# A graph-attention layer on one core: 29 pairs of raw rows instead of 24, with twelve row buffers and reordered group steps

## The chip, the cores and the metric

The kernel runs on one core of a Trainium2 chip. The metric is the time on the device in microseconds (us), from start to end of one execution; lower is better. The engines are called by the names of the profile: PE (TensorE, matrix products), DVE (VectorE), ACT (ScalarE), POOL (GpSimd) and SP (SyncE, which here only issues DMAs). Each engine works through its own queue of instructions in order, and waits on semaphores for others. "L897" is line 897 of the kernel before.

## The reference

`x` has 12500 nodes of 128 features, and there are 400000 edges, sorted by destination, with 32 attributes each. One layer of GATv2 attention with 8 heads and a feed-forward block is computed:

```python
h = relu(layernorm(x))
n1 = ln1(h)
x_l, x_r = n1 @ W_l, n1 @ W_r                    # 8 heads of 16
m = leaky_relu(x_l[src] + x_r[dst] + edge_attr @ W_e, 0.2)   # also one loop per node, with the mean attribute
alpha = einsum('ehc,hc->eh', m, att)
a = softmax of alpha over the edges of each dst
g = h + segment_sum(x_l[src] * a, dst) + bias
out = x + g + gelu(ln2(g) @ W1 + b1) @ W2 + b2
```

## The kernel before, in words

Nodes lie in 98 tiles of 128. Edges are cut into 782 pairs; a pair is two units of 256 edges, so four blocks of 128 edges. The program has a front, a main loop over pairs, and an end. Every order is written out by hand: functions are called round by round under a manual schedule, and each engine's queue has that order.

**The front** (from `make_identity` to `clear(0)`, rounds `r` at L720) loads `x`, normalizes it in groups of four tiles, and writes the rows `x_l` to DRAM (`x_l`, L526 and L534). One group enters per round, and `x_l` of a group comes 8 rounds after it entered. Beside this, three more things are done in the front:

- *Raw rows.* For 24 pairs, one in every 32, `raw_gather` (L268) gathers the rows of `x` by source with four indirect DMAs, issued by POOL, into a tile `raw` with five buffers; three rounds later `raw_store` (L279) stores them through SP to `raw_dram`. Their indices come with one load, `load_raw`.
- *Differences.* `from_first` (L387) turns the destinations into float (`df`), subtracts the first destination of each unit and of each pair on POOL (`dlb`, L392), and stores both tables to DRAM for the main loop. `fits` (L400) computes a flag that the edges have the expected shape; `edge_constants` (L346) builds constants on DVE out of loaded weights, in round 7.
- The row of `x_r` for the first group (`first_xr`).

**The main loop** (`window_edges`, round loop at L1321) handles a pair `c` in stages, one round apart: `gather` (L889) four rounds ahead, `combine` (PE sums z, L939 to L943), `slope` and `bend`, `score`, `lowest`, `weigh` (ACT exponentials), `turn` (PE), `keep_turned` (ACT), `collect` (PE, L1001), `own_heads` (DVE, L1010 and L1016, seven rounds after `combine`), and `put` (L1023), which stores the two units' sums through SP to `state`. `gather` normally issues four indirect DMAs on POOL (L897), each fetching 128 rows of `x_l`. The tile `xs` has 12 buffers, and a buffer becomes free when `collect` has read it. For one of the 24 raw pairs, `gather` is a plain load from `late_dram` through SP instead, and the twelve `raw_steps`, one per round, have computed the pair's `x_l` rows from the raw rows before (on DVE, ACT and PE). `xr_steps` compute `x_r` for a group of four tiles, eight rounds long, once in about 32 rounds. In the first 196 rounds the mean edge attribute is also summed up (`sum_load`, `sum_up`), and the state is cleared in parts.

When all edges of a group of four node tiles are done, the group's steps run, one or more per round, from round `d["round"]` on: `f_load` (0) loads state, `x_l` and `x_r`; then `f_order`, `f_z`, `f_bend`, `f_score`, `f_low` (5), which needs the state, and so on to `f_up`, `f_gelu`, `f_down` (18) and `f_store` (19), which computes the output and issues its store. Groups are at least 23 rounds apart. The last one but one begins in round 764, the last one in round 790, when all 782 pairs have been put.

In each round the calls stand in this order: `f_gelu(1)`, the pair's stages, the sums, the clearing, the steps of groups, `xr_steps`, `raw_steps`, then

```python
        late_stages = (
            (-WAHEAD, windows),
            (LATE + 2, put),
        )
```

so SP finds `put` last, after the loads for the pair three rounds ahead (`windows`, L905 to L918).

Of the kernel before, what the change touches and what calls it, by code (L numbers as in the profile page):

```python
# [13 lines left out]
F32 = mybir.dt.float32  # L14
BF16 = mybir.dt.bfloat16
I32 = mybir.dt.int32
AF = mybir.ActivationFunctionType
OP = mybir.AluOpType
# [3 lines left out]
P = 128  # L22
# [3 lines left out]
K = 4  # L26
# [7 lines left out]
KU = 2  # L34
U = KU * P
UP = 2
# [12 lines left out]
AHEAD = 4  # L49
WAHEAD = 3  # L50
XR_STEPS = 8
RAW_STEPS = 12
BIG = 2.0**126
CAP = 2.0**120
# [50 lines left out]
def edges_per_node(nt, n_edges):  # L105
    return -(-n_edges // (nt * P))
# [7 lines left out]
def xr_round(t0, nt, n_edges):  # L114

    first = (t0 * P - CW) * edges_per_node(nt, n_edges) // U - SPARE
    return first // UP - WAHEAD - XR_STEPS - 1


def raw_pairs(nt, n_edges):  # L120

    n_pr = -(-n_edges // (UP * U))
    at = [xr_round(t, nt, n_edges) + XR_STEPS + 1 for t in range(GN, nt, GN)]
    return [(r + RAW_STEPS + AHEAD + 1, r) for r in at if r + RAW_STEPS + AHEAD + 2 < n_pr]


# [9 lines left out]
def tile_gnn(  # L136
# [118 lines left out]
    src_raw = build.tile([P, len(raw), UP * KU], I32, name="src_raw")  # L255

    def load_raw():
        step = raw[1]["c"] - raw[0]["c"]
        assert all(d["c"] == raw[0]["c"] + i * step for i, d in enumerate(raw))
        nc.sync.dma_start(  # L260
            src_raw,
            bass.AP(
                tensor=src.tensor, offset=src.offset + raw[0]["c"] * UP * KU,
                ap=[[NCH * K, P], [step * UP * KU, len(raw)], [1, UP * KU]],
            ),
        )

    def raw_gather(d):  # L268
        d["x"] = node.tile([P, UP * KU, P], F32, name="raw", bufs=5)
        for j in range(d["n"]):  # L270
            nc.gpsimd.indirect_dma_start(  # L271
                out=d["x"][:, j, :],
                out_offset=None,
                in_=x,
                in_offset=bass.IndirectOffsetOnAxis(ap=src_raw[:, d["i"], j : j + 1], axis=0),
            )
# [97 lines left out]

    df = rng.tile([RP, EP + U + 1], F32, name="df")
    bad = rng.tile([RP, 2], F32, name="bad")

    def last_of_units():
        nc.vector.tensor_copy(lu, dc[:, U - 1 : EP : U])

        u = NUE - 1
        nc.sync.dma_start(
            lu[u // RU : u // RU + 1, u % RU : u % RU + 1],
            bass.AP(tensor=dst.tensor, offset=dst.offset + n_edges - 1, ap=[[0, 1], [1, 1]]),
        )

    def from_first():  # L387
        nc.vector.tensor_copy(df, dc)
        for step, to in ((U, du_dram), (UP * U, dc_dram)):
            de = df[:, 0:EP].rearrange("p (u e) -> p u e", e=step)  # L390
            dlb = rng.tile([RP, EP], BF16, name="dlb", bufs=2)
            nc.gpsimd.tensor_tensor(  # L392
                dlb.rearrange("p (u e) -> p u e", e=step),
                de,
                de[:, :, 0:1].to_broadcast([RP, EP // step, step]),
                op=OP.subtract,
            )
            nc.sync.dma_start(to.rearrange("(p e) -> p e", e=EP), dlb)

    def fits():  # L400
# [303 lines left out]
    with tc.manual_schedule():  # L704
        make_identity(nc, ident)
        count_up()
        for t in xls:
            nc.gpsimd.memset(t[:, :, P:], 1.0)
        load_weights()
        load_x(0, min(GN, NT))  # L710
        load_raw()
        load_x(GN, min(3 * GN, NT - GN))
        for t in range(4 * GN, NT, 14):
            load_x(t, min(14, NT - t))
        load_dst()
        load_consts()
        nc.gpsimd.memset(empty, 0.0)
        nc.gpsimd.memset(empty[:, :, C + 1 : SH], CAP)
        rows_at = [i * 5 // 4 + (3 if i >= 10 else 0) for i in range(len(raw))]
        for r in range(max(max(len(qs), 9) + LAST + 1, rows_at[-1] + 4)):  # L720
            for d, at in zip(raw, rows_at):
                if r == at:
                    raw_gather(d)
                if r == at + 3:
                    raw_store(d)
            if r == 3:
                weights()
            if r == 7:
                edge_constants()
            if r == 8:  # L730
                last_of_units()
            if r == 12:
                from_first()
            if r == 14:
                fits()
            for t in slots(r - 2):
                nc.vector.reciprocal(t, t)
            for t in slots(r - 1):
                nc.scalar.activation(t, t, AF.Sqrt)
            for late, f in node_stages:  # L740
                if 0 <= r - late < len(qs):
                    f(qs[r - late], r)
            if 0 <= r - LAST < len(first_xr):
                first_xr[r - LAST](qs[0])
        clear(0)
# [82 lines left out]
def window_edges(  # L828
# [30 lines left out]
    with ExitStack() as es:  # L859
# [192 lines left out]
        def tiles(name, d, tag=None, bufs=1):  # L1052
            d[name] = fin.tile([P, GN, P], F32, name=f"f_{name}", tag=tag or f"f_{name}", bufs=bufs)
            return d[name][:, 0 : d["n"]]
# [2 lines left out]
            d[name] = ps2.tile([P, EPR], F32, name=ring)  # L1057
            return d[name]

        def f_load(d):  # L1060
            n, ts = d["n"], d["ts"]
            d["st"] = fin.tile([P, 2, GN, SW], F32, name="st", tag="big", bufs=3)
            for i in range(2):
                nc.sync.dma_start(d["st"][:, i, 0:n], state[i].rearrange("(t p h) f -> p t (h f)", p=P, h=H)[:, ts, :])
            d["xl"] = fin.tile([P, GN, XW], F32, name="f_xl")
            nc.sync.dma_start(d["xl"][:, 0:n], xl_t[:, ts, :])
            d["xr"] = fin.tile([P, GN, NS, P], BF16, name="f_xr")
            nc.sync.dma_start(d["xr"][:, 0:n], xs_t[:, ts, :, :])
# [150 lines left out]
        def f_gelu(k):  # L1219
            def gelu(d):  # L1220
                n = d["n"]
                if k == 0:
                    d["gel"] = fin.tile([P, 2, GN * P], F32, name="gel", tag="big", bufs=3)
                nc.scalar.activation(
                    d["gel"][:, k, 0 : n * P], d[f"u{k}"][:, 0 : n * P], AF.Gelu, bias=cols[:, 5 + k : 6 + k]
                )

            return gelu
# [12 lines left out]

        def f_store(d):
            n = d["n"]
            y = tiles("yo", d, "f_b")
            up = d["y"][:, 0 : n * P].rearrange("p (t f) -> p t f", f=P)
            nc.vector.tensor_add(up, up, d["x"][:, 0:n])
            nc.vector.tensor_add(up, up, h_sb[:, d["ts"], :])
            nc.vector.tensor_add(y, up, b2_r[:, None, :].to_broadcast([P, n, P]))  # L1248
            nc.sync.dma_start(out_t[:, d["ts"], :], y)

        stages = (
            (-AHEAD, gather),
# [11 lines left out]
        )  # L1264
        late_stages = (
            (-WAHEAD, windows),
            (LATE + 2, put),
        )
        sum_stages = (
            (0, sum_load),  # L1270
# [1 line left out]
            (3, mean),  # L1272
        )
        SUM_STEP = 2
        early = ((17, f_gelu(1)),)
        steps = (
            (0, f_load),
            (1, f_order),
            (2, f_z),
            (3, f_bend),  # L1280
            (4, f_score),
            (5, f_low),
            (6, f_exp),
            (7, f_den),
            (8, f_out),
            (9, f_h),
            (10, f_stats),
            (11, f_root),
            (12, f_scale),
            (13, f_turn),  # L1290
            (14, f_turned),
            (15, f_up(0)),
            (16, f_up(1)),
            (16, f_gelu(0)),
            (18, f_down),
            (19, f_store),
        )
        GAP = 23
        last_round = n_pr + LATE + 2
        free = SUM_STEP * (NL - 1) + 5  # L1300
        for d, u in zip(groups, done_after(NT, n_edges)):
            d["round"] = max(free, (u // UP if u < NUE else n_pr) + LATE + 2)
            free = d["round"] + GAP
# [14 lines left out]

        CLEAR = 8
        with tc.manual_schedule():  # L1320
            for r in range(-AHEAD, max(last_round, groups[-1]["round"] + 20)):  # L1321
                in_round(r, early)
                for late, f in stages:
                    c = r - late
                    if 0 <= c < n_pr:
                        f(c)
                for late, f in sum_stages:
                    i, off = divmod(r - late, SUM_STEP)
                    if off == 0 and 0 <= i < NL:
                        f(i)  # L1330
                if r > 0 and r % CLEAR == 0 and r // CLEAR < NT // GT:
                    clear(r // CLEAR)
                in_round(r, steps)
                in_round(r, enumerate(xr_steps), qs[1:])
                in_round(r, enumerate(raw_steps), raw)
                for late, f in late_stages:
                    c = r - late
                    if 0 <= c < n_pr:
                        f(c)
# [358 lines left out]
```

## Time and profile before

| what | value |
|---|---|
| median of 3 runs | 4033.95 us (4027.9 to 4034.51) |
| the profiled execution: time, span | 4031.16 us, 4029.0 us |
| busy in the span: PE, DVE, ACT, POOL | 3542.0, 2539.1, 2131.2, 2980.9 us |
| mean granted clock of PE | 0.954 |
| front: start of the first raw gather, start of the last | 6.33, 164.08 us |
| main loop: start of the first gather, of the last | 168.53, 3959.64 us |
| last sum of the last pair begins | 3982.61 us |
| output store of the last group issued | 4023.75 us |

The profile is one execution recorded by the hardware. Its span runs from the first to the last instruction; the time of the execution is some 2 us longer. Busy time of an engine says what it executed, and not what it waited for. For a gather on POOL the record covers the work of issuing, not the landing of the data.

### The profile page before, as it was taken

Reading aid. Unit: us, or ns where it says so; the run is one execution under the profiler, and the core shown is the slowest. Engines: PE = TensorE matmul, PEld = TensorE weight load, DVE = VectorE, ACT = ScalarE, POOL = GpSimd, SP = SyncE. Lnnn points to the kernel's source line nnn. Section 1 sums busy time; section 2 is a strip of 40 time slices with the busy share of each in tenths; the row PEclk is TensorE's granted clock in tenths of the full one; section 3 lists DMA queues with packets and bytes.
Section 4 is the critical chain, followed back from the end, with each engine's and each line's share of the span. In section 5 each row is a group of like instructions: output and inputs, shape, how many; then the busy total and the mean of one; then the engine's idle time right before and its main releaser. Section 6 shows DMA issues by size and latency. Waiting matters only on the chain.

```text
span 4029.0 us, 65580 instructions
## 1 busy us (share of the span) xinstructions
PE 3542.0 (88%) x19059; PEld 2507.7 (62%) x19255; DVE 2539.1 (63%) x5835; ACT 2131.2 (53%) x4638; POOL 2980.9 (74%) x3155
## 2 busy tenths in 40 slices
PE   3488888888899999999999999989999999989986
PEld 2356666666666666666666666666666666666664
DVE  6556666666666666666666666666666665656654
ACT  5544544544455555555465456555555555545553
POOL 6777777777777777777777777777777777777772
PEclk7799999999999999999999999999999999999998
DMA  6778878767666666656666666656666666566562
GB/s 185 207 175 192 193 184 190 174 160 168 164 120 137 124 124 132 125 112 131 131 126 131 126 132 124 128 127 115 124 136 126 125 131 130 111 131 112 120 133 56
DMA packets 646655, 560.85 MB, mean 139 GB/s; under 512 B 384830, under 2 KB 523949, under 8 KB 646045
## 3 DMA queue, kind: packets, MB, share of 16 engines
q1 hardware_dynamic: 545709, 339.00, 33.7%
q0 software_dynamic: 100000, 217.41, 30.4%
q8 instruction: 156, 2.56, 0.3%
q14 instruction: 214, 1.75, 0.2%
q10 hardware_dynamic: 576, 0.13, 0.0%
HBM read 489.80 MB, written 66.32 MB: 138 GB/s over the span
## 4 chain that ended last, share of the span: by engine, by line
PE 38%; POOL 25%; DMA 22%; issue 13%; SPq 1%; DVE 1%; ACT 0%; POOLq 0%; DVEq 0%; ACTq 0%
POOL xs L897 23%; DMA xs<-xl_dram,src_sb 21%; PE z L943 8%; PE acc L1001 8%; PE ab L961 7%; PE pt_ps L987 4%; PE z L939 4%; PE z L942 2%; POOL raw L271 2%; PE ab L960 1%; PE acc L1234 1%; PE acc L1209 1%; SPq L283 0%; DMA state<-rec 0%; DMA dc<-in_dst 0%
## 5 line engine op out<-in xcount | busy, mean ns | idle before, releaser
L897 POOL DMA_INDIRECT xs<-xl_dram,src_sb x3029 | 2868.9, 947 | 923.3 <-issue 792.7
L979 ACT ACTIVATE p<-ab,rec 128x256 f32<-128x256 f32 x1563 | 655.5, 471 | 1055.2 <-DVE rec L968 1039.1
L1010 DVE TENSOR_TENSOR own<-acc,diag 128x272 f32<-128x272 f32 x782 | 343.6, 439 | 1049.5 <-PE acc L1001 1034.9
L1001 PE MATMUL acc<-xs,pt 128*128 128x136 f32 x6250 | 879.8, 285 | 0.2 <-DVE f_yo L1248 0.2
L939 PE MATMUL z<-ident,xs 128*128 128x128 f32 x3125 | 562.6, 283 | 349.9 <-DMA xs<-xl_dram,src_sb 319.2
L939 PEld LDWEIGHTS z<-ident,xs 128*128 128x128 f32 x3125 | 398.7, 142 | 756.6 <-DMA xs<-xl_dram,src_sb 419.8
L943 PE MATMUL z<-ea,we_z 128*128 128x512 f32 x1564 | 839.4, 619 | 0.1
L961 PE MATMUL ab<-m,negrep 128*128 128x512 f32 x1564 | 799.5, 593 | 11.0 <-issue 1.1
L1001 PEld LDWEIGHTS acc<-xs,pt 128*128 128x128 f32 x6250 | 807.1, 196 | 0.4 <-PE pt_ps L987 0.4
L992 ACT COPY pt<-pt_ps 128x512 f32<-128x512 f32 x782 | 455.1, 582 | 619.5 <-PE pt_ps L987 613.8
L987 PEld LDWEIGHTS pt_ps<-ident,p 128*128 128x128 f32 x3125 | 408.6, 146 | 440.8 <-issue 391.2
L968 DVE TENSOR_REDUCE rec<-ab 128x2 f32<-128x512 f32 x781 | 539.7, 691 | 121.8 <-PE ab L961 113.3
L954 DVE TENSOR_TENSOR m<-z,zs 128x512 f32<-128x512 f32 x782 | 532.6, 681 | 127.4 <-ACT zs L949 127.0
L949 ACT ACTIVATE zs<-z 128x512 f32<-128x512 f32 x782 | 472.6, 604 | 41.1 <-DMA ea<-in_ea_t 32.2
L987 PE MATMUL pt_ps<-ident,p 128*128 128x128 f32 x3125 | 490.2, 281 | 1.9 <-ACT p L979 0.9
L1016 DVE TENSOR_REDUCE rec<-own 128x34 f32<-128x272 f32 x782 | 340.9, 436 | 26.7
L943 PEld LDWEIGHTS z<-ea,we_z 128*128 128x128 f32 x1564 | 308.0, 197 | 33.1
L961 PEld LDWEIGHTS ab<-m,negrep 128*128 128x128 f32 x1564 | 300.8, 192 | 37.4 <-issue 1.1
L942 PE MATMUL z<-ne,xrw 128*128 128x512 bf16 (+1 forms) x781 | 305.0, 391 | 0.2 <-issue 0.2
L925 DVE TENSOR_SCALAR ne<-dlw,nid 112x512 bf16<-112x512 bf16 x782 | 290.7, 372 | 14.0 <-DMA dlw<-du_dram 13.9
L960 PE MATMUL ab<-ne,farw 128*128 128x512 bf16 x588 | 225.4, 383 | 0.0
L271 POOL DMA_INDIRECT raw<-in_x,src_raw x96 | 95.6, 996 | 53.3 <-issue 28.5
(198 smaller groups left out, 2232.9 us busy)
## 6 DMA issues: line engine op xcount, KB each, us to landing
dlw<-dc_dram SPq DMA_DIRECT2D x196, 384.0 KB
ea<-in_ea_t SPq DMA_DIRECT2D x196, 256.0 KB
ea_s<-in_ea_t SPq DMA_DIRECT2D x98, 512.0 KB
xs<-xl_dram,src_sb POOLq DMA_INDIRECT x3029
state<-rec SPq DMA_DIRECT2D x1563, 9.0 KB
xrw<-xs_dram SPq DMA_DIRECT2D x782, 24.0 KB
state<-empty SPq DMA_DIRECT2D x28, 504.0 KB
st<-state SPq DMA_DIRECT2D x48, 288.0 KB
```

The source lines that it names most:

```text
L897: nc.gpsimd.indirect_dma_start(out=xs[:, j, :], out_offset=None, in_=xl_dram, in_offset=bass.IndirectOffsetOnAxis(ap=src_sb[:, c * KP + j ...
L939: nc.tensor.matmul(z[:, j * P : (j + 1) * P], d["xs"][:, j, 0:P], ident, start=(j == 0), stop=False, is_transpose=True)
L942: nc.tensor.matmul(z[:, :e], xrw[c % NV], d["ne"][:, :e], start=False, stop=False)
L943: nc.tensor.matmul(z[:, :e], we_z[:, c % QP, :], d["ea"][:, :e], start=False, stop=True)
L949: nc.scalar.activation(d["zs"][:, :e], d["z"][:, :e], AF.Copy, scale=SLOPE)
L954: nc.vector.tensor_tensor(d["m"][:, :e], d["z"][:, :e], d["zs"][:, :e], op=OP.max)
L961: nc.tensor.matmul(ab[:, :e], negrep.rearrange("p n h -> p (n h)"), d["m"][:, :e], start=False, stop=True)
L968: nc.vector.tensor_reduce(d["rec"][:, :, CX], d["ab"].rearrange("p (u e) -> p u e", e=U), AX.X, OP.min)
L979: nc.scalar.activation(d["p"][:, us], d["ab"][:, us], AF.Exp, bias=d["rec"][:, i, CX:SH], scale=-1.0)
L987: nc.tensor.transpose(d["pt_ps"][:, js], d["p"][:, js], ident)
L992: nc.scalar.copy(d["pt"][:, :e], d["pt_ps"][:, :e])
L1001: nc.tensor.matmul(d["acc"][:, i, :], d["pt"][:, j * P : (j + 1) * P], d["xs"][:, j, :], start=(j == js[0]), stop=(j == js[-1]),)
```

## The change

Five further raw pairs are added: for each of the first five, the pair eight rounds later (`RAW_MORE`, `RAW_SHIFT`), so 29 in all; their indices come with a second load. The tile `raw` has 12 buffers, and the raw gathers of the front are placed without the gap of three rounds after the tenth. The differences move from POOL to ACT: 21 activations, three a round in rounds 11 to 17 (`differ`), with the negated first destinations as bias (`nf`, on DVE), and the two stores come in round 18 (`keep_differences`). `last_of_units` moves from round 8 to 9, `from_first` from 12 to 10, `edge_constants` from 7 to 13, `fits` from 14 to 15.

In the main loop `put` comes one round earlier, in the round of `own_heads`. Of a group, the loads of `x_l` and `x_r`, `f_order`, `f_z` and `f_bend` come four rounds ahead of the state's load (`f_state`, a function of its own now), and the steps after it follow without the rounds that those took: `f_low` is two rounds after the state's load, and the last steps come three rounds earlier. The store of the output (`f_put`) is split off from `f_store` and comes one round after it.

```diff
--- before.py
+++ after.py
@@ -49,6 +49,8 @@
 AHEAD = 4
 WAHEAD = 3
 XR_STEPS = 8
+RAW_MORE = 5
+RAW_SHIFT = 8
 RAW_STEPS = 12
 BIG = 2.0**126
 CAP = 2.0**120
@@ -121,6 +123,7 @@
 
     n_pr = -(-n_edges // (UP * U))
     at = [xr_round(t, nt, n_edges) + XR_STEPS + 1 for t in range(GN, nt, GN)]
+    at = at + [r + RAW_SHIFT for r in at[:RAW_MORE]]
     return [(r + RAW_STEPS + AHEAD + 1, r) for r in at if r + RAW_STEPS + AHEAD + 2 < n_pr]
 
 
@@ -255,18 +258,20 @@
     src_raw = build.tile([P, len(raw), UP * KU], I32, name="src_raw")
 
     def load_raw():
-        step = raw[1]["c"] - raw[0]["c"]
-        assert all(d["c"] == raw[0]["c"] + i * step for i, d in enumerate(raw))
-        nc.sync.dma_start(
-            src_raw,
-            bass.AP(
-                tensor=src.tensor, offset=src.offset + raw[0]["c"] * UP * KU,
-                ap=[[NCH * K, P], [step * UP * KU, len(raw)], [1, UP * KU]],
-            ),
-        )
+        step = GN * P * edges_per_node(NT, n_edges) // (UP * U)
+        for part in (raw[: len(raw) - RAW_MORE], raw[len(raw) - RAW_MORE :]):
+            assert all(d["c"] == part[0]["c"] + i * step for i, d in enumerate(part))
+            i = part[0]["i"]
+            nc.sync.dma_start(
+                src_raw[:, i : i + len(part), :],
+                bass.AP(
+                    tensor=src.tensor, offset=src.offset + part[0]["c"] * UP * KU,
+                    ap=[[NCH * K, P], [step * UP * KU, len(part)], [1, UP * KU]],
+                ),
+            )
 
     def raw_gather(d):
-        d["x"] = node.tile([P, UP * KU, P], F32, name="raw", bufs=5)
+        d["x"] = node.tile([P, UP * KU, P], F32, name="raw", bufs=12)
         for j in range(d["n"]):
             nc.gpsimd.indirect_dma_start(
                 out=d["x"][:, j, :],
@@ -374,6 +379,8 @@
 
     df = rng.tile([RP, EP + U + 1], F32, name="df")
     bad = rng.tile([RP, 2], F32, name="bad")
+    nf = rng.tile([RP, RU], F32, name="nf")
+    dlbs = [rng.tile([RP, EP], BF16, name=f"dlb{i}") for i in range(2)]
 
     def last_of_units():
         nc.vector.tensor_copy(lu, dc[:, U - 1 : EP : U])
@@ -386,15 +393,17 @@
 
     def from_first():
         nc.vector.tensor_copy(df, dc)
-        for step, to in ((U, du_dram), (UP * U, dc_dram)):
-            de = df[:, 0:EP].rearrange("p (u e) -> p u e", e=step)
-            dlb = rng.tile([RP, EP], BF16, name="dlb", bufs=2)
-            nc.gpsimd.tensor_tensor(
-                dlb.rearrange("p (u e) -> p u e", e=step),
-                de,
-                de[:, :, 0:1].to_broadcast([RP, EP // step, step]),
-                op=OP.subtract,
-            )
+        nc.vector.tensor_scalar(nf, df[:, 0:EP:U], -1.0, None, op0=OP.mult)
+
+    def differ(i):
+        for dlb, step, us in ((dlbs[0], U, range(UP * i, UP * i + UP)), (dlbs[1], UP * U, (i,))):
+            for u in us:
+                es = slice(u * step, (u + 1) * step)
+                f = u * step // U
+                nc.scalar.activation(dlb[:, es], df[:, es], AF.Identity, bias=nf[:, f : f + 1])
+
+    def keep_differences():
+        for dlb, to in zip(dlbs, (du_dram, dc_dram)):
             nc.sync.dma_start(to.rearrange("(p e) -> p e", e=EP), dlb)
 
     def fits():
@@ -716,8 +725,8 @@
         load_consts()
         nc.gpsimd.memset(empty, 0.0)
         nc.gpsimd.memset(empty[:, :, C + 1 : SH], CAP)
-        rows_at = [i * 5 // 4 + (3 if i >= 10 else 0) for i in range(len(raw))]
-        for r in range(max(max(len(qs), 9) + LAST + 1, rows_at[-1] + 4)):
+        rows_at = [i * 5 // 4 for i in range(len(raw))]
+        for r in range(max(max(len(qs), 9) + LAST + 1, max(12 + RU // UP, 16), rows_at[-1] + 4)):
             for d, at in zip(raw, rows_at):
                 if r == at:
                     raw_gather(d)
@@ -725,13 +734,17 @@
                     raw_store(d)
             if r == 3:
                 weights()
-            if r == 7:
+            if r == 9:
+                last_of_units()
+            if r == 10:
+                from_first()
+            if 0 <= r - 11 < RU // UP:
+                differ(r - 11)
+            if r == 11 + RU // UP:
+                keep_differences()
+            if r == 13:
                 edge_constants()
-            if r == 8:
-                last_of_units()
-            if r == 12:
-                from_first()
-            if r == 14:
+            if r == 15:
                 fits()
             for t in slots(r - 2):
                 nc.vector.reciprocal(t, t)
@@ -1057,11 +1070,14 @@
             d[name] = ps2.tile([P, EPR], F32, name=ring)
             return d[name]
 
-        def f_load(d):
+        def f_state(d):
             n, ts = d["n"], d["ts"]
             d["st"] = fin.tile([P, 2, GN, SW], F32, name="st", tag="big", bufs=3)
             for i in range(2):
                 nc.sync.dma_start(d["st"][:, i, 0:n], state[i].rearrange("(t p h) f -> p t (h f)", p=P, h=H)[:, ts, :])
+
+        def f_load(d):
+            n, ts = d["n"], d["ts"]
             d["xl"] = fin.tile([P, GN, XW], F32, name="f_xl")
             nc.sync.dma_start(d["xl"][:, 0:n], xl_t[:, ts, :])
             d["xr"] = fin.tile([P, GN, NS, P], BF16, name="f_xr")
@@ -1241,12 +1257,14 @@
 
         def f_store(d):
             n = d["n"]
-            y = tiles("yo", d, "f_b")
             up = d["y"][:, 0 : n * P].rearrange("p (t f) -> p t f", f=P)
+            y = d["out"] = tiles("yo", d, "f_b")
             nc.vector.tensor_add(up, up, d["x"][:, 0:n])
             nc.vector.tensor_add(up, up, h_sb[:, d["ts"], :])
             nc.vector.tensor_add(y, up, b2_r[:, None, :].to_broadcast([P, n, P]))
-            nc.sync.dma_start(out_t[:, d["ts"], :], y)
+
+        def f_put(d):
+            nc.sync.dma_start(out_t[:, d["ts"], :], d["out"])
 
         stages = (
             (-AHEAD, gather),
@@ -1264,7 +1282,7 @@
         )
         late_stages = (
             (-WAHEAD, windows),
-            (LATE + 2, put),
+            (LATE + 1, put),
         )
         sum_stages = (
             (0, sum_load),
@@ -1272,32 +1290,34 @@
             (3, mean),
         )
         SUM_STEP = 2
-        early = ((17, f_gelu(1)),)
+        early = ((14, f_gelu(1)),)
         steps = (
-            (0, f_load),
-            (1, f_order),
-            (2, f_z),
-            (3, f_bend),
-            (4, f_score),
-            (5, f_low),
-            (6, f_exp),
-            (7, f_den),
-            (8, f_out),
-            (9, f_h),
-            (10, f_stats),
-            (11, f_root),
-            (12, f_scale),
-            (13, f_turn),
-            (14, f_turned),
-            (15, f_up(0)),
-            (16, f_up(1)),
-            (16, f_gelu(0)),
-            (18, f_down),
-            (19, f_store),
+            (-4, f_load),
+            (-3, f_order),
+            (-2, f_z),
+            (-1, f_bend),
+            (0, f_state),
+            (1, f_score),
+            (2, f_low),
+            (3, f_exp),
+            (4, f_den),
+            (5, f_out),
+            (6, f_h),
+            (7, f_stats),
+            (8, f_root),
+            (9, f_scale),
+            (10, f_turn),
+            (11, f_turned),
+            (12, f_up(0)),
+            (13, f_up(1)),
+            (13, f_gelu(0)),
+            (15, f_down),
+            (16, f_store),
+            (17, f_put),
         )
         GAP = 23
         last_round = n_pr + LATE + 2
-        free = SUM_STEP * (NL - 1) + 5
+        free = SUM_STEP * (NL - 1) + 7
         for d, u in zip(groups, done_after(NT, n_edges)):
             d["round"] = max(free, (u // UP if u < NUE else n_pr) + LATE + 2)
             free = d["round"] + GAP
@@ -1318,7 +1338,7 @@
 
         CLEAR = 8
         with tc.manual_schedule():
-            for r in range(-AHEAD, max(last_round, groups[-1]["round"] + 20)):
+            for r in range(-AHEAD, max(last_round, groups[-1]["round"] + 18)):
                 in_round(r, early)
                 for late, f in stages:
                     c = r - late
```

## The prediction

> **What bounds the kernel now.** I read the page's busy row and cost groups first, then POOL's timeline through the front, then POOL's busy time by stretch of the main loop, then the end on SP's and DVE's timelines.
>
> ```profile
> PE 3542.0 (88%) x19059; PEld 2507.7 (62%) x19255; DVE 2539.1 (63%) x5835; ACT 2131.2 (53%) x4638; POOL 2980.9 (74%) x3155
> ...
> L897 POOL DMA_INDIRECT xs<-xl_dram,src_sb x3029 | 2868.9, 947 | 923.3 <-issue 792.7
> ```
>
> The busy row misleads: PE shows 88%, POOL 74%. But POOL's 3029 gathers have 923 us of idle "before" them, nearly all 0.30 us of issue, which belongs to each gather. Stretches of 100 us, restricted to the gather line (columns: stretch, length, POOL busy and count, PE clock, DMA share, GB/s):
>
> ```profile
> 468.00:568.00 100.00, 75.61 (x81) 0.98 0.83 194
> 2468.00:2568.00 100.00, 75.61 (x81) 0.98 0.66 136
> ```
>
> Every stretch from 168 to 3868 has 80 or 81 gathers: one per 1.25 us, whether the DMA share is 0.83 or 0.6. So nothing holds POOL up, and POOL is the main loop's clock. (3960.58 - 168.53) / 3029 = 1.252 us each; a pair of four costs 5.0 us. PE's own round, where it runs without gaps (3933.5 to 3945.5 in the chain), is 3.95 us.
>
> POOL's timeline in the front (start, duration, what; in brackets the idle before):
>
> ```profile
> 30.22 0.94 POOL L271 DMA_INDIRECT raw<-in_x,src_raw  x1 [0.30 <-issue]
> 53.41 0.94 POOL L271 DMA_INDIRECT raw<-in_x,src_raw  x1 [22.25 <-DMA raw_dram<-raw]
> ...
> 63.39 2.72 POOL L271 DMA_INDIRECT raw<-in_x,src_raw  x1 [0.30 <-issue]
> ...
> 73.90 3.77 POOL L271 DMA_INDIRECT raw<-in_x,src_raw  x1 [0.30 <-issue]
> ...
> 82.69 12.28 POOL L392 TENSOR_TENSOR dlb<-df 112x3584 bf16<-112x3584 f32 x2
> 95.13 1.23 POOL L271 DMA_INDIRECT raw<-in_x,src_raw  x1 [0.16 <-issue]
> ...
> 164.08 0.94 POOL L271 DMA_INDIRECT raw<-in_x,src_raw  x1 [0.30 <-issue]
> ...
> 168.53 0.95 POOL L897 DMA_INDIRECT xs<-xl_dram,src_sb  x1 [0.15 <-POOL xrw L876]
> ```
>
> POOL is the front's bound too: it waits 22 us for a store to free one of five row buffers, spends 12.3 us on two subtractions, and the main loop starts 4.45 us after its last raw gather. The x_l work is over earlier (DVE's last x_l ends at 152.5).
>
> The end, SP's queue, and DVE's last sum:
>
> ```profile
> 3977.74 0.39 SPq L1249 DMA_DIRECT2D out<-f_yo  x1
> 3978.33 10.13 SPq L1023 DMA_DIRECT2D state<-rec  x13
> 3989.57 1.00 SPq L1064 DMA_DIRECT2D st<-state  x2
> 3990.62 0.50 SPq L1066 DMA_DIRECT2D f_xl<-xl_dram  x1
> ```
> ```profile
> 3982.61 0.30 DVE L1016 TENSOR_REDUCE rec<-own 128x17 f32<-128x136 f32 x1
> ```
>
> SP stood 31.3 us at the output of the last group but one (its wait on f_yo), with puts queued behind. They then go one after another, 1.43 us each, and end 6.7 us after the last sum. Then come the state and xl loads (f_xl lands in 4.96 us), z, bend, score; f_low starts at 4001.70.
>
> **The change, part by part.** The sum is against the profiled execution, 4031.16 us (span 4029.0); it lies 2.8 us below the median of 4033.95, which I add at the end.
>
> *Main loop.* Five more pairs are loaded as finished rows: 20 gathers of 1.252 us leave POOL, -25.0 us. Each adds raw_steps. On ACT: two Sqrt table loads and two returns at 1.28, four relus at 0.49, four squares at 0.40 and their accumulator reads, about 9 us; on PE about 2 us (transposes 0.6, products 1.05 and overlap); on DVE about 4 us; on SP five issues of 0.3 to 0.4 counting the front's store. The cover: in 468 to 618, ACT is busy 72 of 150 us; PE's period of 32 rounds needs 32 x 3.95 = 126, plus 2 for xr and 2 to 4 for raw, against 150 on POOL. If that cover were gone, the five pairs would cost PE 10 us. The existing 24 raw pairs show no dent in POOL's 81 per 100 us. Two raw pairs eight rounds apart put PE behind by up to 5 us each, and it gains 1.05 us a round, so it is even before the second.
>
> *Front.* Twelve buffers remove the 22.25 wait (less the usual 0.30: -21.9). The subtractions go to ACT (-12.5 with the stretched gather after them). Twenty raw gathers are added: 20 x 1.249 = +25.0. Net -9.4 us. Checked directly: 6.33 + 115 x 1.249 + 4.6 (the two stretched gathers, which stay) = 154.6 for the last start, +4.45 = 159.0 for the first main gather against 168.53: -9.5. Is POOL ever held by a store now? Pair 17 would start near 91 and needs the store of round 9, on SP at about 60 in this trace; pair 24, near 128, the store of round 18, about 109 here. No. The 21 ACT subtractions: no such row exists; the nearest, 128x256 Exp with a bias at 0.47 and 128x512 Identity at 0.69, give 14 x 0.47 + 7 x 0.69 = 11.4 us. Bounds: 7 us (overlap of neighbours, square's rate) to 15. ACT is nearly full there, so this delays the x_l work; against that, edge_constants no longer stops ACT for 15.2 us (46.91, waiting for late constants; about 5 of DVE work remain), and the 11.63 us stop at 97.81 behind POOL's subtractions goes. So x_l ends at 152.5 - 10 - 11.6 + 11.4 = about 142, at the worst 150, still before POOL's 155. If that cover failed, each us past 155 would be a us of the total. SP gets one more load issue (0.5) and five stores (0.36), waiting on gathers as now.
>
> A rule of the Trainium skill speaks against this. "SBUF — State Buffer", Who interferes with whom: a copy, cast or tensor_scalar of DVE in a two-port mode locks GpSimd out for the whole instruction. The two stretched gathers agree: they end 0.8 us after the cast (63.14 to 65.30) and the custom reduction (72.97 to 76.85). By the rule the 28 gathers that now run beside DVE from 31 to 66, and those beside edge_constants, would lose perhaps 5 us more (twenty operations of 0.2 to 0.3 us), and the front would give -4.5. By the rows, 93 of 96 raw gathers stay below 1.3 us with DVE 86% busy beside them, so short operations don't show. I take the rows: -9.5; bounds -13 (fewer collisions, shorter start) and +3.
>
> *Steps of the groups.* f_load, order, z and bend come four rounds earlier; the state is loaded alone, in round 0; put comes one round earlier, the output store one round after its sum. In the loop this is worth nothing: POOL sets the pace. At the end three things change. (a) gelu (0.69, table returns 1.28), f_down (1.95) and f_store (2.1 on DVE) of the last group but one leave the drain, in which the last pair takes 15.1 us from z (3967.4) to its sum (3982.9); I take 4.5 off. (b) SP no longer stands at that output: of 6.7 us from last sum to state load, one or two put landings remain; -4. (c) From state issue (3989.57) to f_low is 12.1 us; now only the state's landing remains, put at 5.3 by f_xl's 4.96; z, bend and score (2.5 + 1.5 + 1.9) lie beside it. -6.8. Together -15.3; f_down's earlier place may cost PE 1.3 before the last z. I take -14, bounds -8 and -18.
>
> *The added waits.* put now waits on SP for own_heads of its own round. Behind it stand the next round's raw and group loads and windows; place (DVE) needs those three rounds, 15 us, later. And f_low has two rounds after the state load, not five: 10 us against up to 4.8 of waiting for puts (the longest such wait of L1064) and 5 of landing. DVE may stand there a few us per group. The rows have 12 slots: POOL may lead PE's z by about 5 pairs, 25 us, and leads by 6.3 (3923.34 to 3929.66), so some 18 us of lag are free. Taken at zero in the loop; bounds 0 and +10.
>
> Sum: -25.0 - 9.5 - 14 = -48.5; 4031.2 - 48.5 = 3982.7; with 2.8 for the median, 3985.
>
> **The rivals.** *The front keeps its time:* ACT's subtractions and SP's stores make x_l late, and the first main gather stays at 168.5. For: ACT is full from 104 to 134. Against: 12 us of margin as reckoned. 3985 + 9.5 = 3995; chance 0.12. *The five pairs bring little:* in these periods the DMA share is up to 0.83, and if landings slow until PE exhausts the slots, half or more of the 25 is lost: 3985 + 15 = 4000. Against: 81 gathers per 100 us at 0.83. 0.08. *Slower:* SP falls behind through put's wait, the state lands late, and DVE stands at f_low with the whole pipeline. The loop has 24 such groups; it decides when one holds DVE longer than the 18 us of free lag. If each then holds POOL 2.5 us, +60 outweighs -48.5: 4046. For: DVE and SP are in order, and the margin at f_low is near zero. Against: stalls of a few us are below 18. 0.05. *It does not do what it says* (store slots or the loads' order still stop POOL as before, and the pairs' gain is paid in the front): near 4030, 0.03.
>
> **How the numbers follow.** The main case, 0.72, gives 3985, with its own range 3974 to 3998. The range to the first two rivals and the added waits' bound: 3973 to 4008. About 8 us, 0.2%, is what a measurement of this kernel can tell from no change (its three runs span 6.6). Faster 0.92, within it 0.03, slower 0.05.
>
> **What would show it.** Right: 3009 main gathers, still 80 or 81 per 100 us between 200 and 1100; the first near 159; no wait on raw_dram of over 1 us; two or fewer puts after the last sum; f_low about 8 us after it instead of 18.8. Wrong: gaps on POOL in front of L897 or its successor, f_low standing over 10 us for st, x_l ending after 155, or a last gather not 34 us earlier.

## The result, and the profile after

The changed kernel takes 3990.53 us (median of 4 runs, 3988.03 to 3992.54) against 4032.39 us (4 runs, 4027.9 to 4034.51): ratio 0.9897, 95% interval 0.988 to 0.9914, some 42 us faster. The forecast was 3985 with a range of 3973 to 4008. The profiled execution took 3991.79 us with a span of 3990.0, 39.0 less than the span before.

From the page (busy row, then two cost groups: count, then busy time and mean ns of one, then the idle time before them):

```profile
PE 3532.0 (89%) x19110; PEld 2509.8 (63%) x19315; DVE 2547.6 (64%) x5936; ACT 2188.6 (55%) x4769; POOL 2971.8 (74%) x3153
...
L910 POOL DMA_INDIRECT xs<-xl_dram,src_sb x3009 | 2853.8, 948 | 917.0 <-issue 791.8
...
L276 POOL DMA_INDIRECT raw<-in_x,src_raw x116 | 113.9, 982 | 39.0 <-issue 32.9
```

Twenty gathers have left the main loop (L910) and twenty have come to the front (L276): 3029 + 96 = 3009 + 116 = 3125. One gather costs 0.95 us and 0.30 of issue in either place. The stretches of 100 us, restricted to the gather line:

```profile
468.00:568.00 100.00, 75.61 (x81) 0.98 0.80 199
2468.00:2568.00 100.00, 75.62 (x81) 0.98 0.61 125
```

There are 80 or 81 gathers per 100 us as before, also in the periods that hold two raw pairs: POOL is still the loop's clock. POOL's timeline in the front:

```profile
41.65 2.71 POOL L276 DMA_INDIRECT raw<-in_x,src_raw  x1 [0.31 <-issue]
...
80.87 3.49 POOL L276 DMA_INDIRECT raw<-in_x,src_raw  x1 [0.31 <-issue]
...
155.81 0.94 POOL L276 DMA_INDIRECT raw<-in_x,src_raw  x1 [0.31 <-issue]
158.92 0.93 POOL L889 MEMSET xrw<- 128x128 bf16 x6 [2.17 <-issue]
160.01 0.95 POOL L910 DMA_INDIRECT xs<-xl_dram,src_sb  x1 [0.15 <-issue]
```

The 22 us wait for a raw store and the two subtractions are gone; the two stretched gathers have stayed. The first main gather starts at 160.01 instead of 168.53. The end, first on SP's timeline, then the chain of waits (start, duration, what), then DVE's rows for the second instruction of `f_low`, which needs both the state and the score, before and after:

```profile
3937.88 0.39 SPq L1267 DMA_DIRECT2D out<-f_yo  x1
3939.51 10.35 SPq L1036 DMA_DIRECT2D state<-rec  x10
3949.90 0.43 SPq L1082 DMA_DIRECT2D f_xl<-xl_dram  x1
3950.38 0.50 SPq L1084 DMA_DIRECT2D f_xr<-xs_dram  x1
3951.13 5.82 SPq L1036 DMA_DIRECT2D state<-rec  x5
3958.08 0.95 SPq L1077 DMA_DIRECT2D st<-state  x2
```
```profile
3951.13 3.83 DMA state<-rec
...
3955.07 1.42 DMA state<-rec
...
3956.61 1.45 DMA state<-rec
...
3958.58 3.60 DMA st<-state
...
3962.27 0.22 DVE f_mn L1130
```
```profile
4001.70 0.19 DVE L1115 TENSOR_TENSOR f_mn<-f_mn,acc 128x32 f32<-128x32 f32 x1 [1.85 <-PE acc L1104]
```
```profile
3962.59 0.19 DVE L1131 TENSOR_TENSOR f_mn<-f_mn,acc 128x32 f32<-128x32 f32 x1
```

DVE's last sum starts at 3951.33. SP stood 3.2 us at the output of the last group but one, and this instruction of `f_low` follows the issue of the state load by 4.51 us instead of 12.13. But three puts (five stores, one or two for a pair) still end after the last sum, the first of them taking 3.83 us, and just ahead of it stand the two loads `f_xl` and `f_xr`, which the change moved forward.

Span by span: the first main gather comes 8.5 us earlier, first to last main gather takes 3769.77 instead of 3791.11 us (-21.3), and last main gather to end 60.22 instead of 69.36 (-9.1): -39.0 together.

### The profile page after: what moved, and what is told of

Its sections match the earlier page's. It is cut to its first block, busy times and chain, and to the rows that moved or that the text cites. A ratio compares the mean times of both kernels' runs of the same rounds, so it can differ in the third digit from the quotient of the medians.

```text
span 3990.0 us, 65961 instructions
## 1 busy us (share of the span) xinstructions
PE 3532.0 (89%) x19110; PEld 2509.8 (63%) x19315; DVE 2547.6 (64%) x5936; ACT 2188.6 (55%) x4769; POOL 2971.8 (74%) x3153
## 4 chain that ended last, share of the span: by engine, by line
PE 41%; POOL 21%; DMA 21%; issue 12%; DVE 0%; ACT 0%; POOLq 0%; SPq 0%; DVEq 0%; ACTq 0%
POOL xs L910 21%; DMA xs<-xl_dram,src_sb 21%; PE z L956 9%; PE acc L1014 9%; PE ab L974 8%; PE pt_ps L1000 5%; PE z L952 5%; PE z L955 2%; PE ab L973 1%; PE acc L1250 1%; PE acc L1225 1%; PE pt_ps L578 0%; PE acc L1120 0%; PE acc L1103 0%; PE acc L1210 0%
## 5 line engine op out<-in xcount | busy, mean ns | idle before, releaser
L910 POOL DMA_INDIRECT xs<-xl_dram,src_sb x3009 | 2853.8, 948 | 917.0 <-issue 791.8
L276 POOL DMA_INDIRECT raw<-in_x,src_raw x116 | 113.9, 982 | 39.0 <-issue 32.9
```

The costliest lines, as they stand in the source:

```text
L910: nc.gpsimd.indirect_dma_start(out=xs[:, j, :], out_offset=None, in_=xl_dram, in_offset=bass.IndirectOffsetOnAxis(ap=src_sb[:, c * KP + j ...
```

## The experiments

Theory after the result: POOL bounds front and loop alike and its 3125 gathers are conserved, so time is won only where POOL stood (the store wait) or did other work (the subtractions). The pairs are worth time only as filling while x_l is not there. The end is set by the chain of last sum, puts and state load. Rivals: the pairs are worth their 25 us; x_l would have hidden wait and subtractions; the end owes its gain to put's earlier round, or cannot gain more because the puts follow one another anyway. Unless it says otherwise, "the changed kernel" below is its second run, `e2_again` (first main gather 161.26, loop 3766.5, end 60.2 us, ratio 0.9891); "loop" is first to last main gather, "end" is last main gather to the end of the span.

**The front.** Four kernels, each the changed one with one thing undone. The kernel before took 4038.31 us beside them (9 runs, 4031.03 to 4042.98), so they are held against the changed kernel by ratios and by positions in the trace. No added pairs:

```diff
-RAW_MORE = 5
+RAW_MORE = 0
...
+            if not part:
+                continue
```

> The changed kernel without its five added pairs (24 rows of x in the front, 3029 gathers in the main loop; buffers, ACT subtractions and steps as changed). Theory of the prediction's sum (each pair is worth four main gathers, 5.0 us): 25 us longer than the changed kernel, about 4015 us, if its front also kept starting the main loop near 160 us. Theory of conserved gathers (a pair only moves four gathers of POOL from the main loop to the front, 3125 in all either way; it is worth time only while POOL would otherwise wait for x_l): POOL's last raw gather ends near 131 us, x_l at about 142 us then sets the start of the main loop, first main gather at 145 to 148 us, 20 more gathers of 1.253 us after it; so 25 - 13 = +10 to +13 us, about 4002 us. Stretched gathers in the main loop (over 0.965 us): if xr_parts of the added pairs make them, near 75 instead of 97.

Measured: 4002.79 us, ratio 0.9913 (0.99 to 0.9927); by the difference of ratios 7 to 9 us longer than the changed kernel, by span 5.9 and 7.9 against its two profiled executions. POOL's timeline:

```profile
130.65 0.94 POOL L278 DMA_INDIRECT raw<-in_x,src_raw  x1 [0.30 <-issue]
143.25 0.93 POOL L891 MEMSET xrw<- 128x128 bf16 x6 [11.65 <-DMA xl_dram<-xl]
144.33 0.95 POOL L912 DMA_INDIRECT xs<-xl_dram,src_sb  x1 [0.15 <-issue]
```

Here POOL has nothing left to gather at 131.6 and stands 11.65 us for the last x_l store. The 20 extra main gathers lengthen the loop by 21.5 to 24.8 us, and the earlier start gives back 16 to 17. So the five pairs are worth 6 to 9 us, most of the POOL idle time that they fill, and not 25. The stretched main gathers (over 0.965 us; 0.944 is usual) were 81, against 75 in the kernel before and 82 to 100 with added pairs in these two sets: that does not tell whether the added pairs make any.

Three added pairs (RAW_MORE = 3):

> The changed kernel with three added pairs instead of five. Sum of the prediction: two pairs fewer, +10 us, about 4000.5 us. Conserved gathers: POOL's last raw gather ends near 147 us, still after x_l (142 us), first main gather near 150 us, eight more main gathers: 0 us (within 2 us), about 3990.5 us.

Measured: 3993.05 us, ratio 0.9889 (0.9874 to 0.9905); first main gather 149.67, after a last x_l store that SP issued by 142. The time is that of the changed kernel within the intervals, as conservation says; +10 us does not fit the trace either (span 3985.0 against 3988.0 and 3990.0). Pairs four and five bring nothing that can be seen.

Five row buffers:

```diff
-        d["x"] = node.tile([P, UP * KU, P], F32, name="raw", bufs=12)
+        d["x"] = node.tile([P, UP * KU, P], F32, name="raw", bufs=5)
```

> The changed kernel with five row buffers instead of twelve. Prediction's sum: POOL's wait for a raw store, 22 us before, returns in front of the main loop: first main gather at 180 to 184 us, +20 to +24 us, about 4012 us. Rival: the wait was only long because SP's stores stood behind other work that the change also moved, or x_l hides it: +0 to +9 us.

```profile
55.25 0.94 POOL L276 DMA_INDIRECT raw<-in_x,src_raw  x1 [23.79 <-DMA raw_dram<-raw]
```

Measured: 4013.63 us, ratio 0.994 (0.9927 to 0.9954), 17 to 20 us longer; first main gather 180.93, 20 to 21 us later. The wait is back in one piece and nothing hides it.

Subtractions back on POOL:

```diff
-        nc.vector.tensor_scalar(nf, df[:, 0:EP:U], -1.0, None, op0=OP.mult)
+        for dlb, step in ((dlbs[0], U), (dlbs[1], UP * U)):
+            de = df[:, 0:EP].rearrange("p (u e) -> p u e", e=step)
+            nc.gpsimd.tensor_tensor(
+                dlb.rearrange("p (u e) -> p u e", e=step),
+                de,
+                de[:, :, 0:1].to_broadcast([RP, EP // step, step]),
+                op=OP.subtract,
+            )
...
-            if 0 <= r - 11 < RU // UP:
-                differ(r - 11)
```

> The changed kernel with the two subtractions back on POOL (two operations, 12.3 us before) and none on ACT. Prediction's sum: +12.5 us, first main gather near 172.5 us, about 4003 us; x_l would end some 10 us earlier on ACT, which gives nothing, as POOL is the later one. Rival (ACT's subtractions hold up x_l, and x_l holds the start): +2 us or less.

A group of POOL's instructions (columns as in the page's cost groups):

```profile
L398 POOL TENSOR_TENSOR dlb<-df 112x3584 bf16<-112x3584 f32 x2 | 12.3, 6163 | 0.0
```

Measured: 4006.25 us, ratio 0.9921 (0.9908 to 0.9935), 10 to 12 us longer; first main gather 173.86, 12.6 to 13.9 later. The 12.5 is found. A miss: without ACT's subtractions the last x_l store was issued at 149, later than in the changed kernel and not 10 us earlier. It cost nothing, since POOL's last raw gather (169.67) is later still.

The 20 to 21 us of the buffers and the 12.6 to 13.9 of the subtractions, less the 25 of the added gathers, make up the front's gain of 7.3 to 8.5. The moved rounds of `edge_constants`, `fits` and the raw gathers were not undone one by one.

**The end.** The next four ran beside one another; the kernel before took 4033.36 us there (9 runs, 4029.94 to 4034.59).

> The changed kernel itself once more, beside the three that follow, so that each is held against it on one chip. Expected: ratio to the kernel before 0.9897 (0.988 to 0.9914), last gather to end of span near 60 us; the main loop from first to last gather 3770 us, with 80 to 100 stretched gathers.

Measured: 3989.64 us, ratio 0.9891 (0.9876 to 0.9906); end 60.2 us, that of the first run; loop 3766.5 with 92 stretched gathers.

The old order of the groups' steps with the new front:

```diff
-            (LATE + 1, put),
+            (LATE + 2, put),
...
-        early = ((14, f_gelu(1)),)
+        early = ((17, f_gelu(1)),)
...
-            (-4, f_load),
...
             (0, f_state),
-            (1, f_score),
...
-            (16, f_store),
-            (17, f_put),
+            (0, f_load),
+            (1, f_order),
...
+            (19, f_store),
+            (19, f_put),
...
-        free = SUM_STEP * (NL - 1) + 7
+        free = SUM_STEP * (NL - 1) + 5
```

> The changed front (five pairs, twelve buffers, subtractions on ACT) with the old order of the groups' steps: loads, order, z and bend in rounds 0 to 3, put one round later, output put with f_store in round 19. Prediction's sum: +14 us against the changed kernel, all behind the last gather, none in the loop. By the trace of the changed kernel, in which only 9 us of the 14 are found: last gather to end of span 68 to 70 us, against 60; +8 to +10 us. If the earlier state load and the added waits cost the loop something, the loop from first to last gather is shorter here by what they cost: 3 us or more.

```profile
3942.96 0.39 SPq L1267 DMA_DIRECT2D out<-f_yo  x1
3943.88 10.33 SPq L1036 DMA_DIRECT2D state<-rec  x13
3955.31 0.96 SPq L1077 DMA_DIRECT2D st<-state  x2
3956.31 0.51 SPq L1082 DMA_DIRECT2D f_xl<-xl_dram  x1
```

Measured: 3997.71 us, ratio 0.9917 (0.9903 to 0.993), 8.1 us longer by the medians; last gather to end 68.38, 8.2 more. So the moved steps are worth 8 us, all behind the last gather. Nearly all of it lies behind the state load: from its issue to the second instruction of `f_low` it takes 11.7 us here (3955.31 to 3967.00) against 4.2 and 4.5, while last gather to last sum (22.32) lies within the changed kernel's own 21.55 and 22.83. The loop took 3766.0 us, as in the changed kernel's faster execution: a cost of the added waits does not show, in loops that differ by 3 us from one execution to the next.

Load of f_xl and f_xr four rounds earlier still:

```diff
-            (-4, f_load),
+            (-8, f_load),
```

> The changed kernel with the load of f_xl and f_xr eight rounds before the group's round instead of four; all else as it is. Theory (in the changed kernel's end the load lies between the last puts and holds one of them for 3.8 us instead of 1.4): last sum to state load 3.2 to 4.5 us instead of 6.75, no put over 2 us, last gather to end 57 to 58 us; -2 to -3.5 us. Rival (three puts of 1.4 us in a row and their issue are the whole of it): 6 us or more, 0 us.

SP's timeline and the chain:

```profile
3940.57 0.43 SPq L1082 DMA_DIRECT2D f_xl<-xl_dram  x1
3941.05 0.50 SPq L1084 DMA_DIRECT2D f_xr<-xs_dram  x1
3942.55 11.54 SPq L1036 DMA_DIRECT2D state<-rec  x13
3955.22 0.95 SPq L1077 DMA_DIRECT2D st<-state  x2
```
```profile
3950.68 1.42 DMA state<-rec
...
3952.21 1.42 DMA state<-rec
...
3953.75 1.45 DMA state<-rec
...
3955.66 3.43 DMA st<-state
```

The last sum starts at 3951.48. The state load is issued 3.74 us behind it instead of 6.4 to 6.75, each put takes 1.4 us, and last gather to end is 57.35 instead of 60.2. The theory holds with its number: the loads moved forward collided with the last puts and took back some 2.9 us. Other runs repeat it: last sum to state load is 6.4 to 7.5 us in all eight executions of the new order with the load at -4 (seven before the slow set below, and `e3_xr_psum` in it), and 3.7, 4.6 and 4.5 us in the three with it at -8 (`e2_load_early`, `e3_best`, `e3_all`). The median is 3987.14 us, 2.5 less; the ratios, 0.9885 (0.987 to 0.99) and 0.9891, are not told apart by their intervals, the traces tell them apart.

put one round later ((LATE + 2, put)):

> The changed kernel with put one round later (after the windows of round LATE + 2), as before the change. Theory (SP has nothing else to do at the end, the puts follow the sums, each a landing of 1.4 us after the other): last sum to state load within 1 us of 6.75, time within 1 us. Rival (put's earlier round is what takes the puts off SP's queue at the output of the last group but one): four or more puts after the last sum, +1.5 to +4 us.

```profile
3948.91 3.92 DMA state<-rec
```

Measured: 3989.85 us, ratio 0.9895 (0.9879 to 0.991); last sum (3950.83) to state load 6.65, end 60.10. Seven stores follow the loads instead of five, and four puts end after the last sum instead of three, the first of them the one that stands behind the loads and takes 3.92 us. The rival had expected that count, but with 1.5 to 4 us more time, which did not come. So put's earlier round is worth nothing that can be seen by itself.

**A last set, in which every kernel was slower.** In this set all kernels took 18% longer, the kernel before too (4772.27 us, 33 runs, 4761.26 to 4785.83); they are compared with that one alone. The record gives the chip of this set the same number as that of the first set, where the kernel before took 4038.31 us, so that it was another chip is not shown, and why it was slower stays open. Stretches of e3_best by the gather line, then its chain by engine:

```profile
468.00:568.00 100.00, 64.74 (x69) 0.93 0.71 182
2468.00:2568.00 100.00, 64.70 (x69) 0.95 0.49 103
```
```profile
PE 64%; issue 12%; DVE 9%; another core or an unknown queue 7%; ACT 1%; POOL 1%; DMA 1%; SPq 0%; POOLq 0%; DVEq 0%; ACTq 0%
```

There are 69 gathers per 100 us: POOL waits here and PE's side carries the chain, at a granted clock of 0.93 instead of 0.96, with 12% of "issue" and 7% of a releaser that the profile cannot name. What saves POOL's time can then be expected to pay little here.

The kernel before with the added pairs alone:

```diff
+RAW_MORE = 5
+RAW_SHIFT = 8
...
+    at = at + [r + RAW_SHIFT for r in at[:RAW_MORE]]
```

> The kernel before with the five added pairs alone (five row buffers, subtractions on POOL, old steps). Conserved gathers: POOL bounds the front there too (its last raw gather ends after x_l), so the pairs only move 20 gathers across the start of the main loop: first main gather 24 to 27 us later than before (193 to 196 us), 3009 main gathers, 0 us (within 3 us) against the kernel before. If the pairs themselves are worth 25 us: -25 us. If their extra work on ACT and PE costs: +3 us or more.

Measured: 4780.93 us, ratio 1.0019 (1.001 to 1.0028), 9 us slower. First main gather 219.39, with five waits for raw stores on POOL (22.7, 7.3, 3.5, 7.2 and 8.4 us). The gain of 25 did not come in this set. Whether the pairs are worth zero where POOL is the bound this run can't say, nor whether the 9 us are the longer waits or the pairs' work on the other engines: the kernel before has no trace in this set.

Three pairs with the early load (RAW_MORE = 3 and (-8, f_load)):

> The changed kernel with three added pairs instead of five and the load of f_xl and f_xr eight rounds before the group. Worked out from the two runs apart: last gather to end 57.4 us instead of 60.2, front and loop together as changed: -3 us, ratio to the kernel before 0.988 to 0.989. Rival (three pairs alone ran 3 to 5 us shorter than the changed kernel, and that is theirs and not scatter of the stretched gathers): -6 to -8 us.

Measured: 4762.75 us, ratio 0.9979 (0.997 to 0.9988). That is faster than the kernel before by 10 us in this set; the changed kernel itself was not run there, so whether this version beats it stays open. POOL was idle for 28.8 us at the start of the loop, waiting for a raw store behind the late x_l work.

The remainder of xr kept in PSUM:

```diff
-            nc.vector.tensor_sub(tile_of(d, "left", 0), xr, d["parts"][:, :, 0, :])
+            nc.vector.tensor_sub(xr, xr, d["parts"][:, :, 0, :])
+            nc.scalar.copy(d["parts"][:, :, 1, :], xr)
+            nc.vector.tensor_sub(d["parts"][:, :, 2, :], xr, d["parts"][:, :, 1, :])
```

The two operations that made the second and third part in later rounds are left empty.

> The changed kernel with the split of xr done in PSUM: the remainder stays in its PSUM bank, so that the subtraction which makes the third part reads one operand from SBUF and one from PSUM instead of two from SBUF (24 of these, 0.68 us each; in the changed kernel 18 gathers are stretched beside them and lose 7.7 us). Theory (a VectorE operation with both inputs in SBUF keeps GpSimd from writing its descriptors): no gather over 0.965 us beside these operations, main loop from first to last gather 3760 to 3764 us, -4 to -8 us. Rival (it is their output or chance; or PE waits for the bank held longer): 3767 to 3771 us or more, 0 us.

> The three together: three added pairs, loads eight rounds early, the split of xr in PSUM. Sum of the parts: -7 to -11 us against the changed kernel (3 from the end, 4 to 8 from the loop), ratio to the kernel before 0.9865 to 0.9875. If the split in PSUM brings nothing: 0.988 to 0.989.

Measured: 4762.12 us, 0.9981 (0.9971 to 0.9991), and 4762.36, 0.998 (0.9971 to 0.9989): no difference in time to e3_best. The expected ratios and loop times are missed; they were worked out for a loop that POOL bounds, which this set's is not. The mechanism can be read all the same, below under the hardware.

## Why the prediction was right

The profiled executions differ by 39.0 us where the sum said 48.5: some 3.7 are missing in the loop, 1.0 in the front and 4.9 at the end. That the medians miss by 5.5 only has a part of chance in it: the 2.8 us that the prediction added for the median did not come back, since the profiled execution after lies above its median. Of its signs of being right, the gather count, the 81 per 100 us, the start near 159 and the missing wait came. Three puts after the last sum instead of two or fewer, and `f_low` 10 to 11 us behind it instead of 8, did not fit. One sign of being wrong did come: the last gather is 29.9 and 31.9 us earlier in the two executions, not 34.

*Main loop, -25.0.* Found -21.3 and -24.6 in the changed kernel's two profiled executions, -25.1 with the old steps. The count is exact. The rest is stretched gathers, which lost 10.2 us before, and 14.0 and 10.8 in these two executions. The cover held: no dent at two pairs a period.

*Front, -9.5.* Found -8.5 and -7.3. Five buffers give 20 to 21 back (the step said 21.9), subtractions on POOL 12.6 to 13.9 (12.5). ACT's subtractions took 7 groups of some 1.51 us, 10.6 against 11.4; x_l ended at 142 as worked out. The rule of the Trainium skill ("SBUF — State Buffer", Who interferes with whom), that a two-port operation of DVE shuts GpSimd out for its whole length, would have given -4.5 by the prediction's estimate; the rows were nearer, with the same two long-stretched gathers as before. Of the raw gathers before, 94 stay below 1.3 us, not 93, and DVE is busy in 69% of their time, not 86%.

*What those two entries hid.* Read one by one they credit the pairs with 25 us, though the same sum puts 25 us back in the front. The pairs cancel; the net -34.5 is the store wait and the subtractions. The sum was right and could have named the pairs' worth beforehand: without them POOL would end at 131 and wait for x_l, so they are worth that wait, two pairs' time, and pairs beyond it nothing.

*End, -14.* Found -9.1. Here two terms were mis-sized. Step (a), with f_down's price, said -4.5 + 1.3 and brought -1.4 and -0.1. In the first execution the last pair's z to its last sum did fall by 3.5 us (the prediction's 15.1 from 3967.4 to 3982.9 is 15.5), but last gather to last z rose by 2.1. PE is busy for 39.84 of the 40 us from 3908 to 3948 there, so `f_down`, which now stands ahead of the last z, takes its time all the same. Last gather to last sum: 22.97 before, 22.32 with the old steps, 21.55 and 22.83 changed. Step (b), "one or two put landings remain", said -4 and brought -0.2 and -0.6: last sum to state load went from 6.96 to 6.75 and 6.37. It left out that the load moved forward lands among the last puts; with the load out of the way it is 3.74, and the step's size was nearly right. The 31.3 us that the prediction gives for SP at the output of the last group but one are those of the last group's output (to 4023.75); at the last but one SP stood 10.4 us, from 3967.3 to 3977.74. Step (c) said -6.8 and is -7.6: 12.13 to 4.51, both counted to the second instruction of `f_low`, which the prediction's 4001.70 is; its first stands at 3999.65.

*Added waits, zero taken.* None shows. *The rivals:* "the front keeps its time", "slower" and "it does not do what it says" did not happen; "the five pairs bring little" is true of the pairs, but for another reason than landings that slow down, and without its loss to the sum.

## What to carry to other kernels

When one engine's instructions bound two phases, moving them between the phases is worth only the time in which that engine would have stood. Count what is conserved before a count of removed instructions is booked as a gain, and size such filling to the wait (here three pairs did what five did). Moving a load forward, off the critical chain, gives it a new place in a queue: look at what is latency-bound at that new place, here the last puts. Work taken out of a drain helps only if the engine has a gap to put it in.

## What the hardware showed

VectorE operations with both inputs in SBUF stretch GpSimd's indirect gathers. In the changed kernel's first execution (POOL and DVE timelines, the rows between left out):

```profile
2577.80 1.61 POOL L910 DMA_INDIRECT xs<-xl_dram,src_sb  x1 [0.30 <-issue]
2577.91 0.69 DVE L594 TENSOR_TENSOR xr_parts<-xr,xr_parts 128x512 bf16<-128x512 f32 x1
```

The gather ends 0.8 us after the subtraction, 0.67 us late. Beside the 24 such subtractions of a run, 10 to 18 main gathers were stretched in each of the twelve executions that have them, the slow set's too (e3_best: 17), and all but one of these 173 gathers end 0.81 to 0.83 us after the subtraction. With one operand in PSUM the same subtraction keeps its length:

```profile
L590 DVE TENSOR_TENSOR xr_parts<-pt_ps,xr_parts 128x512 bf16<-128x512 f32 (+1 forms) x24 | 16.3, 680 | 15.4 <-issue 7.8 <-ACT xr_parts L589 7.6
```

and beside it not one of the 3009 main gathers was stretched (e3_xr_psum), nor of 3017 (e3_all), though 20 and 19 of the 24 ran beside a gather. A control stands in the changed kernel itself: `m`, of the same length, reads `z` from PSUM, and of 778 that ran beside a gather in its first execution none stood beside a stretched one. The Trainium skill ("SBUF — State Buffer", Who interferes with whom) says that an operation with two SBUF inputs contends with GpSimd's reads, which agrees, and infers that descriptor generation is spared; here a gather that takes its row numbers from SBUF is not. What in the gather is held up, the profile does not show. These gathers lose 3 to 8 us a run outside the slow set; that keeping the remainder in PSUM wins this time there was not measured. Most of the others stand beside the 0.37 us tensor_scalar that makes `ne` (60 to 79 stretched outside the slow set, 4.6 to 6.5 us in all, beside some 780 of them): a short operation delays a gather only now and then.
